# A state space layer with two states per scan instruction: a zero-decay column, an extra copy and fixed PSUM banks

## The chip, the cores and the metric

One of the eight cores of one Trainium2 chip runs the whole program. The metric is device time in microseconds (us), the median of several runs. Engines are named as the profile names them: PE (matmul), DVE (VectorE), ACT (ScalarE), POOL (GpSimd). Every kernel's time here is the median of four runs in the fast state, compared with runs of the kernel before on the same chip in the same rounds. The experiments ran on several chips; the kernel before took 8367 to 8369 us on each of them, so times of different experiments may be set side by side. The kernel places its tiles in one of two memories, SBUF or PSUM (`space=PSUM` in the code).

## The reference, cut to what matters

Two layers follow each other. The second (a windowed attention) is not touched by the change. The first is a selective state space layer over 4 sequences of 4096 positions, with 768 channels and 16 states per channel. Its heart is a recurrence along the sequence:

```python
def step(h, inp):
    dt_t, B_t, C_t, x_t = inp
    dA = jnp.exp(dt_t[:, :, None] * A[None])
    dBx = (dt_t * x_t)[:, :, None] * B_t[:, None, :]
    h = dA * h + dBx
    y_t = jnp.einsum('bdn,bn->bd', h, C_t)
    return (h, y_t)
```

## The kernel before

A sequence is cut into chunks of T = 256 positions, 64 chunks ("steps") in all. In a step 768 channels are 6 tiles of 128 partitions, and 16 states are 4 groups of 4: 24 groups (m) per step. A group is worked off in two halves of two states, so a step has 48 slots. The product dtx = dt * x is made by POOL, once per tile of channels and step; ACT copies it to PSUM (`dtx_ps`) for the products on DVE. The work of a group:

```python
def driven(I, m, h, eng):                 # db = dt * x * B, on DVE (15 of 24) or POOL (9 of 24)
    d, g = divmod(m, NS // NG)
    db = w2.tile([P, NG, T], F32, tag="db", name=f"db_{I}_{m}", bufs=6)
    dtx = dtx_ps[:, d % 2, :] if eng is nc.vector else h["dtx"][d]
    eng.tensor_tensor(db, dtx.unsqueeze(1).broadcast_to([P, NG, T]), h["B"][g], ALU.mult)
    dbs[I, m] = db

def decay(I, m, half, h):                 # da = exp(dt * A), on ACT into PSUM, two buffers
    d, g = divmod(m, NS // NG)
    da = ps_a.tile([P, 2, T], F32, tag="da", name="da")
    for k in range(2):
        n = g * NG + 2 * half + k
        act(da[:, k, :], h["dt"][d // 2][:, d % 2, :], AF.Exp, scale=nega[:, d, n : n + 1])
    das[I, m, half] = da

def scans(I, m, half, hs):                # h = da * h + db, on DVE, one state at a time
    ...
    for k in range(2):
        ...
        nc.vector.tensor_tensor_scan(hs[:, j, :], da[:, k, :], dbs[I, m][:, j, :],
                                     state[:, d, n : n + 1] if I % NCHUNK else 0.0, ALU.mult, ALU.add)

def with_c(I, m, h, hs):                  # last column kept as next chunk's start, then times C, on POOL
    d, g = divmod(m, NS // NG)
    nc.gpsimd.tensor_copy(state[:, d, g * NG : (g + 1) * NG], hs[:, :, T - 1])
    nc.gpsimd.tensor_tensor(hs, hs, h["C"][g], ALU.mult)
```

Everything else of the layer (projections, convolution, layer norm, softplus, gating) is hung into the 48 slots by hand-written tables. The order of instructions on each engine is exactly the order in which this loop writes them:

```python
for half in range(2):
    decay(*nxt, ...)                      # ACT: the decays of the next slot
    if half == 0:
        with_c(*behind[-1])               # POOL: the group before
        ...
    scans(I, m, half, hs)                 # DVE: this slot
    run(I, 2 * m + half, 2 * m + half + 1)   # whatever the tables put into this slot
```

Of the kernel before, what the change touches and what calls it, by code (L numbers as in the profile page):

```python
# [14 lines left out]
P = 128  # L15
C = 384
# [32 lines left out]
def two_layers(  # L49
# [221 lines left out]
    def layer0(x1s, mvs, gms1):  # L271

        with ExitStack() as es:
            es.enter_context(tc.manual_schedule(engines=in_step))
            ps_a = es.enter_context(tc.tile_pool(name="ps_a", bufs=2, space=PSUM))
            ps_x = es.enter_context(tc.tile_pool(name="ps_x", bufs=1, space=PSUM))
            ps_y = es.enter_context(tc.tile_pool(name="ps_y", bufs=1, space=PSUM))
            ps = es.enter_context(tc.tile_pool(name="ps0", bufs=4, space=PSUM))
            bc = es.enter_context(tc.tile_pool(name="bc", bufs=4))
            w1 = es.enter_context(tc.tile_pool(name="w1", bufs=1))  # L280
            w2 = es.enter_context(tc.tile_pool(name="w2", bufs=2))
            gms, gbs, st1s = {}, {}, {}
            dtx_ps = ps_x.tile([P, 2, T], F32, name="dtx_ps")

            def group_norm(b, mv):

# [15 lines left out]
            def next_batch(b, at):  # L302

                st = small.tile([P, NJ, NXT, 6], F32, tag="st0", name=f"st0_{b + 1}")
                mv = small.tile([P, NJ, 2], F32, tag="mv0", name=f"mv0_{b + 1}")
                h = {}

                def load(t, j):
                    h["x"] = w1.tile([P, TX], F32, tag="xs", name=f"xs_{b}_{t}_{j}")
                    nc.sync.dma_start(  # L310
                        h["x"], x[b + 1, j * P : (j + 1) * P, t * TX : (t + 1) * TX]
                    )

                def aggregate():
                    for j in range(NJ):
                        nc.vector.bn_aggr(mv[:, j, :], st[:, j, :, :])

                for n in range(NJ * NXT):
                    t, j = divmod(n, NJ)
                    at(24 * n + 14, lambda t=t, j=j: load(t, j))  # L320
                    at(24 * n + 26, lambda t=t, j=j: nc.vector.bn_stats(st[:, j, t, :], h["x"]))
                end = 24 * NJ * NXT + 24
                at(end, aggregate)
                for n, part in enumerate(group_norm(b + 1, mv)):
                    at(end + 2 + 3 * n, part)
# [4 lines left out]
            def normed(I, h, at):  # L330
# [38 lines left out]

                at(12, load)  # L370
                at(22, by_group)
                at(24, lambda: mean("xn", "mu"))
                at(26, lambda: with_row("mu", ALU.subtract))
                at(30, square)
                at(31, lambda: mean("sq", "var"))
                at(34, root)
                at(35, lambda: with_row("var", ALU.mult))

            def in_proj(pb, k, m, xn):

# [18 lines left out]
            def prepared(I, h, at):  # L399
# [19 lines left out]
                    for k in range(2):  # L419
                        at(slots[k], lambda k=k: one(k))  # L420

                at(-11, kept)
                for p, (x, c, z) in enumerate((
                    ((-10, -9, -6), (1, 2, 5), (9, 10, 13)),
                    ((-6, -5, -2), (3, 4, 7), (12, 13, 16)),
                    ((-4, -3, 0), (7, 8, 11), (15, 16, 19)),
                )):
                    d = 2 * p
                    pair(("x", p), x, lambda pb, k, d=d: in_proj(pb, k, d + k, h["xn"]))
                    at(x[2], lambda p=p, d=d: with_bias(  # L430
                        xb[:, d : d + 2, KC - 1 :], h["pb"][("x", p)], binp[:, d : d + 2]
                    ))

                    def conv_out(p=p, d=d):
                        c = w2.tile([P, 2, T], F32, tag="xc", name=f"xc_{b}_{i}_{d}", bufs=6)
                        with_bias(c, h["pb"][("c", p)], cvb[:, d : d + 2])
                        h["xc"].append(c)

                    pair(("c", p), c, lambda pb, k, d=d: conv(pb, k, d + k))
                    at(c[2], conv_out)  # L440

                    def z_out(p=p, d=d):
                        z = w2.tile([P, 2, T], F32, tag="sz", name=f"sz_{b}_{i}_{d}", bufs=6)
                        with_bias(z, h["pb"][("z", p)], binp[:, ND + d : ND + d + 2])
                        h["sz"].append(z)

                    pair(("z", p), z, lambda pb, k, d=d: in_proj(pb, k, ND + d + k, h["xn"]))
                    at(z[2], z_out)
# [27 lines left out]
                        nc.sync.dma_start(t, src.unsqueeze(0).broadcast_to([P, NG, T]))  # L476
                        h[tag].append(t)

                at(26, burst)
                at(28, lambda: x_proj((0, 1, 2)))  # L480
                at(29, lambda: x_proj((3, 4, 5)))
                at(32, rows)

                def softplus(q, first):

# [41 lines left out]
                    at(first + 6, lost)  # L527
                    at(first + 7, added)

                for q, first in enumerate((34, 36, 46)):  # L530
                    softplus(q, first)

            dbs, das = {}, {}

            def dt_x(I, d, h):
                h["dtx"][d] = w2.tile([P, T], F32, tag="dtx", name=f"dtx_{I}_{d}")
# [3 lines left out]
                )  # L540

            def dt_x_copied(d, h):
                nc.scalar.copy(dtx_ps[:, d % 2, :], h["dtx"][d])

            def driven(I, m, h, eng):

                d, g = divmod(m, NS // NG)
                db = w2.tile([P, NG, T], F32, tag="db", name=f"db_{I}_{m}", bufs=6)
                dtx = dtx_ps[:, d % 2, :] if eng is nc.vector else h["dtx"][d]
                eng.tensor_tensor(  # L550
                    db, dtx.unsqueeze(1).broadcast_to([P, NG, T]), h["B"][g], ALU.mult
                )
                dbs[I, m] = db

            def decay(I, m, half, h):

                d, g = divmod(m, NS // NG)
                da = ps_a.tile([P, 2, T], F32, tag="da", name="da")
                for k in range(2):
                    n = g * NG + 2 * half + k  # L560
                    act(da[:, k, :], h["dt"][d // 2][:, d % 2, :], AF.Exp, scale=nega[:, d, n : n + 1])
                das[I, m, half] = da

            def scans(I, m, half, hs):

                d, g = divmod(m, NS // NG)
                da = das.pop((I, m, half))
                for k in range(2):
                    j = 2 * half + k
                    n = g * NG + j  # L570
                    nc.vector.tensor_tensor_scan(  # L571
                        hs[:, j, :], da[:, k, :], dbs[I, m][:, j, :],
                        state[:, d, n : n + 1] if I % NCHUNK else 0.0,
                        ALU.mult, ALU.add,
                    )

            def with_c(I, m, h, hs):

                d, g = divmod(m, NS // NG)
                nc.gpsimd.tensor_copy(state[:, d, g * NG : (g + 1) * NG], hs[:, :, T - 1])  # L580
                nc.gpsimd.tensor_tensor(hs, hs, h["C"][g], ALU.mult)  # L581

            def summed(I, m, h, hs):


                d, g = divmod(m, NS // NG)
                if d % 2 == 0 and g == 0:
                    h["yt"][d // 2] = ps_y.tile([P, 2, 2, P], F32, tag="y", name="y")
                y = h["yt"][d // 2]
                for k in range(NG):  # L590
                    first = g == 0 and k == 0
                    last = g == NS // NG - 1 and k == NG - 1
                    for half in range(2):
                        nc.tensor.matmul(  # L594
                            y[:, d % 2, half, :], hs[:, k, half * P : (half + 1) * P], ident,
                            is_transpose=True, start=(first and half == 0 and d % 2 == 0),
                            stop=(last and half == 1 and d % 2 == 1), skip_group_check=True,
                        )

            def turn(I, p, h, at, s):  # L600


                def out():
# [21 lines left out]
                    h["yg"].append(yg)  # L625

                at(s, out)
                at(s + 1, back)
                at(s + 4, gated)

            def out_proj(I, h, at):
                b, i = divmod(I, NCHUNK)
# [34 lines left out]
                            nc.vector.bn_aggr(mvs[b][:, m, :], st1s[b][:, m, :, :])  # L667

                at(10, reload)
                for n, slot in enumerate((17, 18, 19, 20, 22, 23)):  # L670
                    m, part = divmod(n, 2)
                    at(slot, lambda m=m, part=part: tile_part(m, range(3 * part, 3 * part + 3)))
                at(26, lambda: residual(0, 2))
                at(28, lambda: residual(2, 1))
                at(30, stats)


# [6 lines left out]
            def slot_of(I):  # L684
# [7 lines left out]
            driven_at = (  # L692
                (-4, 0), (-1, 1), (1, 1), (2, 1), (4, 0), (7, 1), (8, 0), (10, 1),
                (12, 0), (15, 1), (17, 1), (18, 1), (20, 0), (22, 1), (24, 0), (26, 1),
                (26, 1), (26, 1), (30, 0), (33, 1), (36, 0), (39, 1), (40, 0), (43, 1),
            )
            dt_x_at = (-5, 2, 10, 18, 22, 34)

            for I in range(STEPS):
                h = steps[I]  # L700
                for p in range(ND // 2):
                    turn(I, p, h, slot_of(I), (p + 1) * (SLOTS // 3) + 4)
                out_proj(I, h, slot_of(I + 1))
                prepared(I, h, slot_of(I - 1))
                normed(I, h, slot_of(I - 2))
# [32 lines left out]
            behind = []  # L738
            for n in range(STEPS * M):
                I, m = divmod(n, M)  # L740
                hs = w2.tile([P, NG, T], F32, tag="hs", name=f"hs_{I}_{m}", bufs=5)
                for half in range(2):
                    if 2 * n + half + 1 < len(halves):
                        nxt = halves[2 * n + half + 1]
# [420 lines left out]
```

## Time and profile before

| | before |
|---|---|
| time, median | 8367 us |
| state space layer: one step of 64 | 92.3 us |
| attention layer, from 6020 us on | 2338 us |
| DVE busy in the layer, per step | 90.6 us (98%) |
| POOL, PE, ACT busy, per step | 84.9, 78.2, 72.6 us |

How the step and busy times are read, and the lines that they come from, stands in the prediction.

### The profile page before, as it was taken

To read this page: it belongs to the slowest core of one execution; us is meant where nothing else is said; L and a number is where in the kernel's file an instruction comes from. 1 tells how busy PE (TensorE), PEld (TensorE's weight loads), DVE (VectorE), ACT (ScalarE), POOL (GpSimd) and SP (SyncE) were. 2 spreads that over 40 slices of the span, in tenths; PEclk is the share of its full clock that TensorE was granted. 3 is DMA by queue.
4 is the path that set the end of the run, shared out by engine and by line. 5 is a ranking of instruction groups with operands and counts; after the bars stand their busy time and mean duration, and the time that the engine had idled before them with its cause. 6 is when DMAs were issued, how large, how long until landed. Compare 5 with 4: busy or idle time off the path is not lost. (4 is left out here: it accounts for less than half of the span.)

```text
span 8357.8 us, 139186 instructions
## 1 busy us (share of the span) xinstructions
PE 7252.0 (87%) x45882; PEld 5495.0 (66%) x45882; DVE 7311.7 (87%) x13300; ACT 5812.2 (70%) x13758; POOL 7092.7 (85%) x5719
## 2 busy tenths in 40 slices
PE   7888888888888888888888888888699999999999
PEld 5776677777666677776777677766555555555555
DVE  5999999999999999999999999999856666666666
ACT  5777777777777777777777777777545455455455
POOL 4999999999999999999999999999767677777677
PEclk9998898889889998899898889989799999999999
DMA  3111211121112111211211111112122232232222
GB/s 112 59 61 66 75 58 55 63 74 58 62 66 74 53 58 66 72 58 64 68 63 53 58 65 60 55 57 71 65 89 86 76 94 88 78 92 85 83 87 65
DMA packets 327504, 583.06 MB, mean 70 GB/s; under 512 B 62940, under 2 KB 211180, under 8 KB 326660
## 3 DMA queue, kind: packets, MB, share of 16 engines
q1 hardware_dynamic: 326788, 574.17, 21.3%
q8 instruction: 370, 6.06, 0.3%
q14 instruction: 346, 2.83, 0.1%
HBM read 471.49 MB, written 84.73 MB: 67 GB/s over the span
## 5 line engine op out<-in xcount | busy, mean ns | idle before, releaser
L571 DVE TENSOR_TENSOR_SCAN hs<-da,state,db 128x256 f32<-128x256 f32 x5760 | 3855.0, 728 | 88.9 <-ACT da L96 64.8
L96 ACT ACTIVATE da<-dt,nega 128x256 f32<-128x256 f32 x6144 | 2917.7, 477 | 1208.2 <-DVE hs L571 1100.8
L581 POOL TENSOR_TENSOR hs<-hs,C 128x1024 f32<-128x1024 f32 x1536 | 3621.7, 2358 | 123.9 <-POOL state L580 0.4
L594 PE MATMUL y<-ident,hs 128*128 128x128 f32 x12288 | 1774.6, 296 | 904.5 <-POOL hs L581 902.3
L594 PEld LDWEIGHTS y<-ident,hs 128*128 128x128 f32 x12288 | 1540.5, 153 | 1207.9 <-POOL hs L581 1098.9
L941 POOL TENSOR_SCALAR sg<-sg,rsum 128x308 f32<-128x308 f32 x1536 | 1619.9, 1073 | 633.8 <-DVE rsum L939 631.8
L550 POOL TENSOR_TENSOR db<-dtx,B 128x1024 f32<-128x1024 f32 x576 | 1360.5, 2362 | 0.1
L550 DVE TENSOR_TENSOR db<-dtx_ps,B 128x1024 f32<-128x1024 f32 x960 | 1141.3, 1199 | 0.0
L382 PE MATMUL mm_ps<-xn,w_in 128*128 128x256 f32 x4608 | 1127.4, 392 | 10.1 <-DVE yg L624 8.1
L96 ACT ACTIVATE sg<-sg,mx 128x308 f32<-128x308 f32 x1536 | 828.7, 541 | 251.3 <-DVE mx L926 236.7
L926 DVE CUSTOM_DVE_ANT_0 sg<-lg_ps,bias 128x308 f32<-128x308 f32 x1536 | 643.1, 475 | 375.1 <-PE lg_ps L920 375.1
L382 PEld LDWEIGHTS mm_ps<-xn,w_in 128*128 128x128 f32 x4608 | 872.5, 197 | 119.1 <-DVE yg L624 8.4
L389 PE MATMUL mm_ps<-xb,dcv 128*128 128x256 f32 x3072 | 783.9, 409 | 0.0
L389 PEld LDWEIGHTS mm_ps<-xb,dcv 128*128 128x128 f32 x3072 | 615.7, 208 | 88.3 <-issue 0.3
L969 ACT COPY tb<-pt_ps 88x512 f32<-88x512 f32 x384 | 222.2, 579 | 624.7 <-PE pt_ps L965 624.7
L580 POOL COPY state<-hs 128x4 f32<-128x4 f32 x1536 | 289.1, 188 | 341.8 <-DVE hs L571 328.0
L639 PE MATMUL mm_ps<-yg,w_out 128*128 128x256 f32 x2304 | 539.8, 385 | 0.0
L956 DVE COPY ta<-pt_ps 110x512 f32<-110x512 f32 x768 | 492.4, 682 | 23.2 <-PE pt_ps L951 23.2
L639 PEld LDWEIGHTS mm_ps<-yg,w_out 128*128 128x128 f32 x2304 | 439.6, 195 | 59.1
L951 PE MATMUL pt_ps<-ident,sg 128*110 128x128 f32 x3072 | 417.7, 279 | 0.8 <-POOL sg L941 0.8
L951 PEld LDWEIGHTS pt_ps<-ident,sg 128*110 128x110 f32 x3072 | 322.7, 133 | 77.9 <-issue 47.6
L824 PE MATMUL mm_ps<-xn,w_qkv 128*128 128x512 f32 (+2 forms) x612 | 270.7, 579 | 60.4 <-DVE xn L811 53.2
(141 smaller groups left out, 9152.5 us busy)
## 6 DMA issues: line engine op xcount, KB each, us to landing
B<-bcrows SPq DMA_DIRECT2D x256, 512.0 KB
C<-bcrows SPq DMA_DIRECT2D x256, 512.0 KB
vw<-vd SPq DMA_DIRECT2D x1792, 33.0 KB
xr<-x SPq DMA_DIRECT2D x28, 1056.0 KB
vd<-v SPq DMA_DIRECT2D x280, 96.0 KB
xi<-in_x_dram SPq DMA_DIRECT2D x64, 384.0 KB
xo<-in_x_dram SPq DMA_DIRECT2D x64, 384.0 KB
x<-xo SPq DMA_DIRECT2D x64, 384.0 KB
```

Of the source, the lines that this page charges most:

```text
L96: ins = nc.scalar.activation(o, i, func, **kw)
L382: nc.tensor.matmul(pb[:, k, :], w_in[:, j, m * P : (m + 1) * P], xn[:, j, :], start=(j == 0), stop=(j == NJ - 1),)
L389: nc.tensor.matmul(pb[:, k, :], dcv[:, d, c, :], xb[:, d, c : c + T], start=(c == 0), stop=(c == KC - 1),)
L550: eng.tensor_tensor(db, dtx.unsqueeze(1).broadcast_to([P, NG, T]), h["B"][g], ALU.mult)
L571: nc.vector.tensor_tensor_scan(hs[:, j, :], da[:, k, :], dbs[I, m][:, j, :], state[:, d, n : n + 1] if I % NCHUNK else 0.0, ALU.mult, ALU.add,
L581: nc.gpsimd.tensor_tensor(hs, hs, h["C"][g], ALU.mult)
L594: nc.tensor.matmul(y[:, d % 2, half, :], hs[:, k, half * P : (half + 1) * P], ident, is_transpose=True, start=(first and half == 0 and d % ...
L639: nc.tensor.matmul(h["po", first][:, m - first, :], w_out[:, d, m * P : (m + 1) * P], h["yg"][d // 2][:, d % 2, :], start=(d == 0), stop=( ...
L926: nc.vector.tensor_tensor_reduce(sg[:, hh, :], lg[:, :NK], bias[:, 4 * m + hh, :], -1.0, BIG, ALU.add, ALU.min, mx[:, hh : hh + 1],)
L941: nc.gpsimd.tensor_scalar(sg[:, hh, :], sg[:, hh, :], rs[:, hh : hh + 1], None, ALU.mult)
L951: nc.tensor.transpose(pt[: KN[c], col : col + P], sg[:, 2 * pair + hh, KOFF[c] : KOFF[c] + KN[c]], ident,)
L956: nc.vector.tensor_copy(t[: KN[0], :, :].rearrange("p a q -> p (a q)"), pt[: KN[0], :])
```

## The change

The change wants to pay half as often what a scan instruction costs beyond its columns: about 0.11 us, an estimate from two spacings of back-to-back scans, 0.645 us for 256 columns before and 1.18 for 513 in e1_defer. Two states are laid one behind the other with one column between them: a decay of 0 in that column wipes out the first state, and the drive (db) in that column holds the second state's starting value. One scan of 2 x 256 + 1 = 513 columns then does both. For that, the tiles get a gap of one column per pair, the starting value must be copied into each db, and a decay pair takes 513 columns of PSUM, one more than before. In the change each of the two pair buffers has a fixed tile of 4 x 256 columns, which it shares with a copy of dtx, and the pool for everything else shrinks from four buffers to three. A bank is here what the kernel's helper `bank` hands out, a PSUM tile of 2 x 256 columns; a fixed tile counts as two. Some slots were moved to fit the three banks.

```diff
-            ps = es.enter_context(tc.tile_pool(name="ps0", bufs=4, space=PSUM))
+            ps = es.enter_context(tc.tile_pool(name="ps0", bufs=3, space=PSUM))
+            pairs = [ps_a.tile([P, 4 * T], F32, name=f"pair_{k}") for k in range(2)]
+            dtx_ps = [t[:, 0:T] for t in pairs]
+            da_ps = [t[:, T : 3 * T + 1] for t in pairs]
+            for t in da_ps:
+                nc.vector.memset(t[:, T : T + 1], 0.0)
...             (driven)
-                db = w2.tile([P, NG, T], F32, tag="db", name=f"db_{I}_{m}", bufs=6)
+                db = w2.tile([P, 2, 2 * T + 1], F32, tag="db", name=f"db_{I}_{m}", bufs=6)
                 eng.tensor_tensor(
-                    db, dtx.unsqueeze(1).broadcast_to([P, NG, T]), h["B"][g], ALU.mult
+                    states(db), dtx.unsqueeze(1).unsqueeze(1).broadcast_to([P, 2, 2, T]),
+                    h["B"][g].rearrange("p (a k) t -> p a k t", k=2), ALU.mult,
                 )
+                kept = state[:, d, g * NG : (g + 1) * NG].rearrange("p (a k) -> p a k", k=2)
+                nc.scalar.copy(db[:, :, T : T + 1], kept[:, :, 1:2] if I % NCHUNK else zeros)
                 dbs[I, m] = db
...             (scans)
-                for k in range(2):
-                    ...
-                    nc.vector.tensor_tensor_scan(hs[:, j, :], da[:, k, :], dbs[I, m][:, j, :], ...)
+                nc.vector.tensor_tensor_scan(
+                    hs[:, half, :], da_ps[half], dbs[I, m][:, half, :],
+                    state[:, d, n : n + 1] if I % NCHUNK else 0.0, ALU.mult, ALU.add,
+                )
...             (tables: some 50 entries moved by one to seven slots, for example)
-                at(26, burst)
+                at(27, burst)
-                for q, first in enumerate((34, 36, 46)):
+                for q, first in enumerate((35, 37, 43)):
```

## The prediction

> **What bounds the kernel now.** I read the page first for the engines by time, then the stretches of the state space layer, then its groups, then the timeline.
>
> ```profile
> PE   7888888888888888888888888888699999999999
> DVE  5999999999999999999999999999856666666666
> ACT  5777777777777777777777777777545455455455
> POOL 4999999999999999999999999999767677777677
> ```
>
> Two layers: slices 1 to 29 are the state space layer (the scans start at 114 us and end at 6020 us), the rest is the attention, which the diff leaves alone. The first consists of 64 equal steps, (6020 - 114) / 64 = 92.3 us each. A stretch from its middle (columns: PE, PE weight load, DVE, ACT, POOL busy) says how full each engine is:
>
> ```profile
> 1000.00:3000.00 2000.00, 1694.25 (x8876) 1405.86 (x8875) 1963.95 (x2867) 1572.01 (x3442) 1838.58 (x1383) 0.89 0.19 64
> ```
>
> Per step: DVE 1963.95 / 2000 x 92.3 = 90.6 us, POOL 84.9, PE 78.2, ACT 72.6. DVE is the bound, with 1.7 us idle per step, and POOL is close. What fills them:
>
> ```profile
> L571 DVE TENSOR_TENSOR_SCAN hs<-da,state,db 128x256 f32<-128x256 f32 x5760 | 3855.0, 728 | 88.9 <-ACT da L96 64.8
> L96 ACT ACTIVATE da<-dt,nega 128x256 f32<-128x256 f32 x6144 | 2917.7, 477 | 1208.2 <-DVE hs L571 1100.8
> L581 POOL TENSOR_TENSOR hs<-hs,C 128x1024 f32<-128x1024 f32 x1536 | 3621.7, 2358 | 123.9 <-POOL state L580 0.4
> L550 POOL TENSOR_TENSOR db<-dtx,B 128x1024 f32<-128x1024 f32 x576 | 1360.5, 2362 | 0.1
> L550 DVE TENSOR_TENSOR db<-dtx_ps,B 128x1024 f32<-128x1024 f32 x960 | 1141.3, 1199 | 0.0
> ```
>
> A step has 24 groups of four states in 48 slots (half a group, two states). Per slot ACT makes two decays (da), DVE scans them. Per group DVE (15 of 24) or POOL (9 of 24) makes the scan's input db, and POOL multiplies the result by C. da has two buffers, so ACT is never more than one slot ahead. The timeline around slot 20:
>
> ```profile
> 3018.66 0.99 ACT L96 ACTIVATE da<-dt,nega 128x256 f32<-128x256 f32 x2 [0.67 <-DVE hs L571]
> 3018.69 0.19 POOL L580 COPY state<-hs 128x4 f32<-128x4 f32 x1
> ...
> 3018.96 2.36 POOL L581 TENSOR_TENSOR hs<-hs,C 128x1024 f32<-128x1024 f32 x1
> ...
> 3020.37 1.90 ACT L96 ACTIVATE da<-dt,nega 128x256 f32<-128x256 f32 x4
> 3021.29 2.36 POOL L550 TENSOR_TENSOR db<-dtx,B 128x1024 f32<-128x1024 f32 x1
> 3021.45 1.39 DVE L571 TENSOR_TENSOR_SCAN hs<-da,state,db 128x256 f32<-128x256 f32 x2 [0.25 <-POOL hs L581]
> ```
>
> Slot 19's scans end at about 3018.6; POOL then multiplies by C and only then makes a db, done at 3023.65, 5.05 us later. Nobody minds: that db is for four slots later, ACT has made the decays of slots 22 and 23 at 3020.37, and DVE scans slot 22 at 3021.45.
>
> [...] a scan of 256 that starts from a constant takes 667 ns, a tensor_tensor of 512 takes 666. [...] five scans take 3.29 us, (3.29 - 0.73) / 4 = 0.64 apart (0.645 over several such runs)[...]. [...] in 1000 to 6000 us ACT stands 40.7 us before dtx_ps for POOL's dtx, and no later instruction passes it. [...]
>
> **The change, part by part.** (1) Two scans of 256 become one of 513: [...] 1.181 us instead of 2 x 0.645 = 1.290. Saved 0.109 x 48 = 5.2 us a step, so DVE work goes from 90.6 to 85.4 (adding up its instructions at back-to-back spacings I get 86.4, and use that below). (2) POOL and DVE write and read tiles with a gap; counts and element numbers are unchanged, so I expect unchanged durations. (3) Moved slots and one PSUM bank less: PE has 14 us a step spare, I count nothing. (4) Each db gets its starting state by a copy of 128x2 on ACT, 24 a step, about 0.2 us each (from ACT operations on 32x1 at 0.20 to 0.24): 4.8 us of ACT work, which alone would do no harm.
>
> But where it stands does harm. In the built program's order the copy waits for the whole db of the same slot s, though it writes other columns, and the decays of slot s+2 stand behind it. So ACT, whose lead is one slot, now waits for a product that used to have several slots of time.
>
> POOL slots. From the end of scan s-1: 0.06 (semaphore: scan's end to state copy) + 4.96 (3018.69 to 3023.65 above) + 0.06 + 0.20 copy + 0.99 decays + 0.06 = 6.33 us until scan s+2 may start. In it DVE has two scans, 2.36, and what else stands in slots s-1 to s+1 (db 1.14 back to back, other operations from their rows: 0.66, 0.93, 1.05, 1.33 for two). Other ACT work between the copy and the decays adds to the chain. Chain minus cover: slot 4: 6.33 - 2.73 (statistics, 0.37 on average) = 3.6; slot 8: 7.15 (two activations, 0.82) - 3.5 (a db) = 3.65; 12: 6.33 - 3.02 (gating) = 3.3; 20: 6.33 - 2.36 = 3.95; 24: 6.33 - 3.02 (residual) = 3.3; 30: 7.15 (the square) - 3.4 (statistics) = 3.75; 36: 6.33 - 3.3 (layer norm) = 3.0; 40: 8.4 (softplus on ACT, 2.1) - 5.5 (a db, gating, softplus) = 2.9; 44: 6.33 - 5.5 (a db, softplus) = 0.8. Sum 28.3 us a step.
>
> DVE slots. The copy can start 0.06 after the db; copy and decays 1.25 later DVE has run one scan, 1.18: nearly even. With other ACT work behind the copy there is a stall: about 1.4 around slot 47 (softplus), 0.6 and 1.0 around slots 13 to 15, 0.6 at 33, 0.5 elsewhere. The worst is slot 27: two copies wait for two DVE products, and behind them stands the burst of table load, six Silu and table load, 5.8 us (3029.46 to 3035.28), which used to run beside three DVE products; then 0.99 of decays, against 0.93 + 0.37 + 1.18 of DVE work: 4.7 us. Sum 8.8.
>
> Step: 86.4 + 28.3 + 8.8 = 123.5; walking all 48 slots in order by hand with these durations gave 124.1. Difference to 92.3: 31.8 us, times 64 = 2035. 8366 + 2035 = 10,400 us.
>
> **The rivals.** A, the intended one: the copies cost nothing on the path and DVE stays the bound: 8366 - 64 x 5.2 = 8030. For it: DVE is 98% busy and every saved us counts now. Against: the waits above. B, POOL takes over: state copy plus product takes 2.60 (3018.69 to 3021.29), so 24 x 2.60 + 9 x 2.36 + 6 x 0.73 (dtx) = 88.0 a step; with 86 on DVE and few buffers between them I would take 88 to 90, 8090 to 8220. Same objection. C, only the DVE products' waits bite, because POOL's db comes in time: 86.4 + 8.8 = 95 a step, 8550. Against: slot 20 above, where POOL's db cannot start before the multiplication that needs scan s-1. D, the long scan over two PSUM banks or POOL on gapped tiles is slower than I assume: 0.1 us more per scan is 4.8 a step, some 300 us on top.
>
> **Range and chances.** The stall sum of 37 us rests on about 25 chains; I give it 4 to 6 us for latencies, the unseen copy and POOL's gapped access, times 64: 400 us either way. Range 10,000 to 10,850. The direction hangs on one reading, that ACT really stands before the POOL product: faster by over 2% 0.03, within 2% 0.03, slower 0.94.
>
> **What would show it.** A step near 124 us; DVE and POOL each about 69% busy in the layer, ACT near 62%. The scan's row: 3072 of 513 at about 1.25 us, some 2,300 us idle before it, ended by ACT. The new copy's row: 1536, some 0.2 us, about 22 us a step (1,400 in all) idle before it, ended by POOL db. POOL rows at 2.36 us. I am wrong if the copy's wait for POOL is small, or if the scan's mean is well over 1.3 us; the attention should keep its 2,330 us.

## The result, and the profile after

The changed kernel takes 10,202 us (median of 4 runs, 10,198 to 10,203), the kernel before 8367 us. The ratio is 1.219, with a 95% interval of 1.217 to 1.221; it is slower by 22%. Ratios here and below are the mean time of one kernel's fast runs over that of the other's fast runs of the same rounds, so not quite the ratio of the medians quoted.

The share of each engine in 40 equal slices of the changed kernel's span (tenths busy) answers to the four rows of before:

```profile
PE   6777767777777777777777777777776999999999
DVE  5777777777777777777777777777776666666666
ACT  4666666666666666666666666666664454545455
POOL 3666666666666666666666676666666676777777
```

In the state space layer, now nearly 31 slices long, no engine is above seven or eight tenths: no engine is full any more, and a chain of waits sets the time. One stretch of it in numbers (time; PE, PE weight load, DVE, ACT and POOL busy; granted clock, DMA share, GB/s):

```profile
1000.00:3000.00 2000.00, 1435.36 (x6754) 1155.53 (x6753) 1454.16 (x1396) 1233.01 (x3014) 1371.91 (x1053) 0.81 0.14 48
```

The first scan starts at 117.2 us, the last ends at 7856.4, so a step takes 120.9 us. DVE is busy for 1454.16 / 2000 x 120.9 = 87.9 us of it, 2.7 less than before, and idle for 33.0, which was 1.7. The attention layer takes 2344 us, about as before (2338). The groups of the changed kernel (busy us, mean ns; idle before, and who ended it):

```profile
L587 DVE TENSOR_TENSOR_SCAN hs<-pair,state,db 128x513 f32<-128x513 f32 x2880 | 3641.5, 1279 | 1890.9 <-ACT pair L96 1610.6
L600 POOL TENSOR_TENSOR hs<-hs,C 128x1024 f32<-128x1024 f32 x1536 | 3480.2, 2266 | 124.4 <-POOL state L596 1.6
L96 ACT ACTIVATE pair<-dt,nega 128x256 f32<-128x256 f32 x6144 | 2865.4, 474 | 202.7 <-DVE hs L587 99.5
...
L569 ACT COPY db<-state 128x2 f32<-128x2 f32 x1440 | 278.8, 194 | 2528.8 <-POOL db L563 1356.8
...
L563 POOL TENSOR_TENSOR db<-dtx,B 128x1024 f32<-128x1024 f32 x576 | 1354.4, 2351 | 0.1
...
L563 DVE TENSOR_TENSOR db<-pair,B 128x1024 f32<-128x1024 f32 x960 | 1153.7, 1208 | 53.5 <-ACT pair L96 52.9
```

Two columns have changed places. Before, ACT stood idle for 1208 us before its decays (1101 of them ended by DVE's scans), and DVE for 89 us before its scans: ACT ran ahead and stood at the end of its lead. Now it is 203 us before the decays and 1891 us before the scans (1611 of them ended by decays). What ACT waits for has moved to a new row, the copy of 128x2: 0.19 us of work and 2529 us of idle time before it. The list of waits over the whole run splits that by who ended it (total, times, longest; it counts the copies of the first chunk too):

```profile
DVE hs L587 <- ACT pair L96: 1718.6, 995, 5.9
ACT db L569 <- POOL db L563: 1445.0, 576, 3.9
ACT db L569 <- DVE db L563: 1238.5, 896, 2.6
```

All 576 copies behind a POOL product waited, 2.5 us each. The timeline at slot 20, the same place that the prediction shows for before:

```profile
4046.48 0.19 POOL L596 COPY state<-hs 128x4 f32<-128x4 f32 x1 [1.27 <-DVE hs L587]
4046.75 2.26 POOL L600 TENSOR_TENSOR hs<-hs,C 128x1024 f32<-128x1024 f32 x1
...
4048.45 0.38 ACT L550 COPY pair<-dtx 128x256 f32<-128x256 f32 x1
4048.86 1.23 DVE L587 TENSOR_TENSOR_SCAN hs<-pair,db 128x513 f32<-128x513 f32 x1 [1.20 <-ACT pair L550]
4048.97 2.36 POOL L563 TENSOR_TENSOR db<-dtx,B 128x1024 f32<-128x1024 f32 x1
...
4051.36 0.19 ACT L569 COPY db<-zeros 128x2 f32<-128x2 f32 x1 [2.54 <-POOL db L563]
4051.46 1.89 ACT L96 ACTIVATE pair<-dt,nega 128x256 f32<-128x256 f32 x4
...
4052.53 1.23 DVE L587 TENSOR_TENSOR_SCAN hs<-pair,db 128x513 f32<-128x513 f32 x1 [2.45 <-ACT pair L96]
```

The chain can be read from top to bottom: the end of slot 19's scan releases POOL (4046.48), POOL multiplies by C and then makes db (until 4051.33), that releases ACT's copy (4051.36), behind it stand the decays of slot 22 (4051.46, the first pair done at about 4052.45), and they release slot 22's scan (4052.53). From the end of slot 19's scan, 4046.42, that is 6.11 us; the prediction had 6.33. The line at 4048.86 shows a second, smaller wait that the prediction had not named: the scan of slot 21 waited 1.20 us for the copy of dtx, which now lies in its tile. Over the whole run DVE's scans wait 194 us for such copies.

### The profile page after: what moved, and what is told of

Same layout as the page of the kernel before. It is cut to its first block, busy times and chain, and to the rows that moved or that the text cites. A ratio compares the mean times of both kernels' runs of the same rounds, so it can differ in the third digit from the quotient of the medians.

```text
span 10201.6 us, 137884 instructions
## 1 busy us (share of the span) xinstructions
PE 7836.8 (77%) x45882; PEld 5838.4 (57%) x45882; DVE 7139.0 (70%) x10231; ACT 5944.6 (58%) x15294; POOL 6985.1 (68%) x5719
## 5 line engine op out<-in xcount | busy, mean ns | idle before, releaser
L587 DVE TENSOR_TENSOR_SCAN hs<-pair,state,db 128x513 f32<-128x513 f32 x2880 | 3641.5, 1279 | 1890.9 <-ACT pair L96 1610.6
L600 POOL TENSOR_TENSOR hs<-hs,C 128x1024 f32<-128x1024 f32 x1536 | 3480.2, 2266 | 124.4 <-POOL state L596 1.6
L96 ACT ACTIVATE pair<-dt,nega 128x256 f32<-128x256 f32 x6144 | 2865.4, 474 | 202.7 <-DVE hs L587 99.5
L616 PE MATMUL y<-ident,hs 128*128 128x128 f32 x12288 | 1980.3, 319 | 791.9 <-POOL hs L600 599.9
L616 PEld LDWEIGHTS y<-ident,hs 128*128 128x128 f32 x12288 | 1727.2, 167 | 1195.1 <-POOL hs L600 810.4
L569 ACT COPY db<-state 128x2 f32<-128x2 f32 x1440 | 278.8, 194 | 2528.8 <-POOL db L563 1356.8
L387 PE MATMUL mm_ps<-xn,w_in 128*128 128x256 f32 x4608 | 1322.3, 438 | 312.5 <-ACT xb L96 246.9
L563 DVE TENSOR_TENSOR db<-pair,B 128x1024 f32<-128x1024 f32 x960 | 1153.7, 1208 | 53.5 <-ACT pair L96 52.9
L464 PE MATMUL mm_ps<-xc,w_xp 128*56 128x256 f32 x768 | 284.0, 525 | 395.7 <-ACT xc L96 395.7
L661 PE MATMUL mm_ps<-yg,w_out 128*128 128x256 f32 x2304 | 536.9, 383 | 31.8 <-ACT sz L96 31.7
L544 POOL TENSOR_TENSOR dtx<-dt,xc 128x256 f32<-128x256 f32 x384 | 279.2, 727 | 278.6 <-DVE dt L525 278.6
```

What stands on the lines that cost most here:

```text
L96: ins = nc.scalar.activation(o, i, func, **kw)
L387: nc.tensor.matmul(pb[:, k, :], w_in[:, j, m * P : (m + 1) * P], xn[:, j, :], start=(j == 0), stop=(j == NJ - 1),)
L563: eng.tensor_tensor(states(db), dtx.unsqueeze(1).unsqueeze(1).broadcast_to([P, 2, 2, T]), h["B"][g].rearrange("p (a k) t -> p a k t", k=2) ...
L587: nc.vector.tensor_tensor_scan(hs[:, half, :], da_ps[half], dbs[I, m][:, half, :], state[:, d, n : n + 1] if I % NCHUNK else 0.0, ALU.mult ...
L600: nc.gpsimd.tensor_tensor(by_state, by_state, h["C"][g].rearrange("p (a k) t -> p a k t", k=2), ALU.mult)
L616: nc.tensor.matmul(y[:, d % 2, half, :], hs[:, k // 2, at : at + P], ident, is_transpose=True, start=(first and half == 0 and d % 2 == 0), ...
```

## The experiments

Twelve kernels ran. All are correct on these inputs and all their profiles are of the fast state. Runs e1 to e6 and e11 ask what the loss is made of, the others whether a version of this idea beats the kernel before.

### e1_defer: the copy three slots or one slot later

The theory is that the copy's place, and not the copy, is what costs. This run keeps every instruction and moves the copies.

```diff
-                kept = state[...]; nc.scalar.copy(db[:, :, T : T + 1], ...)     # in driven
+            def started(I, m): ... nc.scalar.copy(dbs[I, m][:, :, T : T + 1], ...)
+                    slot_of(I)(slot + (1 if vector else 3), lambda I=I, m=m: started(I, m))
```

> The changed kernel, but the scalar engine's copy of the starting state is put three slots later where GpSimd makes the db and one slot later where VectorE does, so that it no longer stands ahead of decays that are needed at once. Same instructions, another place. Theory W (the wait of the copy is the whole loss): the 28 us a step in which ACT stood before db falls below 4 us, DVE is busy about 95% or more, a step is 88 to 91 us, 8100 to 8300 us in all, 0 to 3% faster than before. Rival L (long scans over two banks, one PSUM bank less and the moved slots cost most of it): stays above 9000.

Measured: 8463 us, ratio 1.011 (1.010 to 1.013). Of the 1835 us lost, 1739 came back by moving 24 copies of two columns per step. ACT's waits before them fell to 129 us in the stretch from 1000 to 6000 us. But the expected gain over the kernel before is missing: it is 1.1% slower, not up to 3% faster. So theory W holds for nearly all of the loss of 22%, and something else takes what the merged scans should have saved: a step takes 93.8 us, not 88 to 91. Where DVE waits in that stretch:

```profile
DVE hs L592 <- ACT pair L96: 160.4, 265, 1.8
DVE hs L592 <- ACT pair L550: 126.2, 156, 1.3
DVE db L563 <- ACT pair L96: 58.1, 53, 1.4
```

### e3_defer_pool and e11_defer_vec: one kind of copy alone

The same edit with `(0 if vector else 3)` and with `(1 if vector else 0)`.

> Only the copies behind GpSimd's products (9 of 24 a step) are three slots later; those behind VectorE's products stay where the change has them. Theory W with the sums of the prediction: removes the 28 us a step of the GpSimd chains and leaves about 9 to 12, so a step of 95 to 101 us, 8550 to 8950 us. Rival V (the copies behind VectorE's products, which hold ACT 19 us a step in the trace, are as bad as GpSimd's): above 9300 us.

Measured: 8929 us, ratio 1.067. Moving POOL's nine copies alone gets 1273 us back, 19.9 us a step. It lies inside the expected 8550 to 8950 and rules out rival V.

> The counterpart of e3_defer_pool: only the copies behind VectorE's products are one slot later, those behind GpSimd's stay. Theory W: GpSimd's chain of about 6 us from one scan to the scan three slots on stays nine times a step; the trace of the changed kernel charges VectorE's copies with the smaller part, so 9550 to 9950 us. If the two kinds of copies were equally bad: near 9000.

Measured: 9877 us, ratio 1.180. Moving DVE's fifteen copies alone gets 326 us back, 5.1 us a step. The two gains add up to 1599 us, together they give 1739: what is under the longer wait shows only when that wait is gone. A reader of the waits list alone would have been misled here. It charges DVE's copies with 1238 us, nearly as much as POOL's 1445, but moving these copies alone gains only 326. The author's estimate of the reason, which no run tests by itself: ACT waits for a DVE product while DVE, the engine that it feeds, is busy with that product, and only what DVE then waits for ACT counts.

### e4_swap: the copy before the product

```diff
+                nc.scalar.copy(db[:, :, T : T + 1], kept[:, :, 1:2] if I % NCHUNK else zeros)
                 eng.tensor_tensor(states(db), ..., ALU.mult)
-                nc.scalar.copy(db[:, :, T : T + 1], kept[:, :, 1:2] if I % NCHUNK else zeros)
```

> The copy stays in its slot but is issued before the product db instead of after it, so the product waits for the short copy and not the copy for the long product. Theory W: no long wait stands before ACT; what remains is that VectorE's or GpSimd's product may wait for ACT to come to the copy, some tenths of a us for 15 of 24 groups: 8100 to 8450 us. If the loss were in the long scans, the banks or the slots: above 9000.

Measured: 8545 us, ratio 1.021 (1.019 to 1.023), outside the expected 8100 to 8450. Swapping two statements gets back 1657 us, so the direction of the wait was the fault. DVE's products now wait for the copy, 198 us in the stretch from 1000 to 6000 us, about 0.25 us each. That is the size that was expected; the range was missed because the gain over the kernel before is missing here as in e1_defer.

### e2_split: the change without its two main parts

Layout, banks, tables and slots as in the change, but two scans of 256 per half and no copies.

```diff
+                for k in range(2):
+                    n = g * NG + 2 * half + k
+                    cut = slice(k * (T + 1), k * (T + 1) + T)
+                    nc.vector.tensor_tensor_scan(hs[:, half, cut], da_ps[half][:, cut],
+                        dbs[I, m][:, half, cut], state[:, d, n : n + 1] ..., ALU.mult, ALU.add)
```

> The changed kernel with its layout, fixed banks, three-bank table and moved slots, but again two scans of 256 per half with their own starting states, and without the copies. Theory W: everything else of the change is about free, so within 1.5% of the kernel before, 8240 to 8490 us, DVE bound at 97 to 98%. Rival L: layout, banks or slots cost by themselves, over 8500 us.

Measured: 8562 us, ratio 1.023. Rival L was right about this part: what the change does around the scans costs 2.3% by itself, some 194 us or 3.0 us a step. Against it e1_defer, which has long scans and well-placed copies, is only 99 us faster, 1.5 us a step. DVE's work did fall as meant. The stretch from 1000 to 3000 us of e2_split, and then of e1_defer:

```profile
1000.00:3000.00 2000.00, 1639.39 (x8539) 1359.09 (x8538) 1910.66 (x2765) 1513.32 (x3313) 1728.87 (x1332) 0.88 0.19 62
```

```profile
1000.00:3000.00 2000.00, 1654.55 (x8723) 1374.75 (x8721) 1849.48 (x1802) 1594.61 (x3888) 1758.82 (x1357) 0.90 0.19 62
```

A step is 95.4 us in e2_split and 93.8 in e1_defer (first scan to last, divided by 64), so DVE is busy for 91.1 and 86.7 us. The scans saved 4.4 us of work a step, and 2.8 of them came back as idle time (4.3 against 7.1). The two runs differ in the copies too: no run has two scans of 256 and well-placed copies, so what the 24 copies themselves cost is not shown.

### e5_before_slots: only the moved slots and the smaller pool

The kernel before, with `bufs=3` for the pool and all slots of the change, nothing else.

> The kernel before with nothing of the change but its moved slots and the table of three PSUM banks instead of four; dtx keeps its own bank, decays their two rotating banks, contiguous tiles. What is open: e2_split, which has the whole change but long scans and copies, came out 2.3% slower than before (8562 against 8368). Theory B (the loss there is the shared tile: dtx lies in the tile of a decay, so copy, product, decay and scan wait for each other): this run is within 0.7% of before, 8310 to 8430. Rival S (the moved slots and the missing bank cost it): about as slow as e2_split, 8500 to 8600.

Measured: 8487 us, ratio 1.015 (1.013 to 1.016). Theory B had expected no loss, rival S all of it; neither is right. Slots and the missing bank cost 120 us, the rest of e2_split's 194 us, 75 us, comes with the layout and the shared tile. Slots and bank were changed together, so the run does not say which of the two it is: with three banks the slots of before were not tried. Its trace shows the added waiting around ACT: in 1000 to 6000 us DVE's scans wait 126 us for decays, which was 68, and ACT waits 146 us for dtx before its dtx copies, which was 41.

This run also separates an effect of layout. POOL's multiplication, in contiguous tiles at the slots of the change:

```profile
L581 POOL TENSOR_TENSOR hs<-hs,C 128x1024 f32<-128x1024 f32 x1536 | 3622.5, 2358 | 123.9 <-POOL state L580 0.2
```

It takes 2358 ns as before; in all runs with the gapped layout and dtx in PSUM that were read for it (the changed kernel, e1_defer, e2_split) it takes 2266 to 2273. Why is not shown.

### e6_split_parity and e7_defer_parity: keep dtx out of the way of the next decay

Five products and four dtx copies are moved by one slot, so that a product no longer reads the tile that the decays of the slot after next overwrite.

```diff
-                (-4, 0), (-1, 1), (1, 1), (2, 1), (4, 0), (7, 1), ...  (18, 1) ... (39, 1), (40, 0), (43, 1),
+                (-4, 0), (-1, 1), (1, 1), (3, 1), (4, 0), (6, 1), ...  (19, 1) ... (38, 1), (40, 0), (42, 1),
+            copied_at = (-2, 5, 12, 21, 24, 37)
```

> e2_split, with five of VectorE's products and four of the dtx copies moved by one slot, so that no product reads the tile which the decays of the next slot but one overwrite, and no copy goes into the tile that the next scan reads. Theory B: ACT's waits for a product (432 us in 5000) nearly vanish and the time falls by 80 to 200 us against e2_split, 8360 to 8480. Rival S: unchanged within 40 us of 8562.

Measured: 8565 us, no change from 8562. ACT's wait for the product, 432 us in 5000, is gone from the list, and the time did not move: theory B failed. In its place ACT waits longer for scans, 905 us instead of 587, so removing that wait by these moves gains nothing. DVE's waits in e6_split_parity, same stretch:

```profile
DVE db L563 <- ACT pair L96: 119.6, 250, 1.5
DVE hs L586 <- ACT pair L96: 62.6, 169, 0.9
```

They sum to 182 us. In e2_split it was 81 (scan for dtx copy) + 61 (scan for decay) + 46 (product for decay) = 188. In both runs somebody waits for the shared tile, and the moved slots only change whom.

> e1_defer with the same moves of products and dtx copies as e6_split_parity. Theory B: VectorE's idle time of 7 us a step halves, 8200 to 8330 us, faster than before by 0.5 to 2%. Rival S: 8420 to 8500 as e1_defer.

Measured: 8486 us, ratio 1.014, against 8463 of e1_defer; theory B failed again. The same picture: the scans no longer wait for the dtx copy, but the products now wait 149 us for decays, which was 58.

### e8_defer_sbuf: dtx from SBUF

```diff
-                dtx = dtx_ps[d % 2] if eng is nc.vector else h["dtx"][d]
+                dtx = h["dtx"][d]
-                    slot_of(I)(slot + 2, lambda d=d, h=h: dt_x_copied(d, h))
```

> e1_defer, but VectorE takes dtx from SBUF and the copies of dtx into PSUM are left out, so nothing but decays is in the paired banks. Theory B: the waits between copy, product, decay and scan are gone, 6 ACT copies a step less; 8150 to 8300 us if products of two SBUF operands neither get longer nor hold GpSimd up. If they do [...], the multiplication on GpSimd gets longer than 2.27 us on average and the time stays above 8350.

Measured: 9133 us, ratio 1.092, the second case of the expectation. The groups of e8_defer_sbuf:

```profile
L605 POOL TENSOR_TENSOR hs<-hs,C 128x1024 f32<-128x1024 f32 x1536 | 3606.6, 2348 | 123.8 <-POOL state L601 0.2
...
L563 DVE TENSOR_TENSOR db<-dtx,B 128x1024 f32<-128x1024 f32 x960 | 1908.3, 1993 | 0.0
...
L563 POOL TENSOR_TENSOR db<-dtx,B 128x1024 f32<-128x1024 f32 x576 | 1486.9, 2581 | 0.1
```

DVE's product took 1208 ns in e1_defer with one operand in PSUM and takes 1993 with both in SBUF, and POOL's product went from 2361 to 2581. The spread says more (shortest, median and longest in ns):

```profile
L563 DVE TENSOR_TENSOR db<-dtx,B x960: 1189/2094/3354, 112.7 to 6775.4; 128x1024 f32<-128x1024 f32 x192
```

At its shortest it is as short as with PSUM (1197 in the changed kernel), at its longest 2.2 us longer, about the time of one multiplication on POOL (2.27 in e1_defer). With both operands in SBUF the product costs 0.8 us more on average here; what holds it up is not shown. Of the two runs the one with dtx in PSUM is faster (8463 us against 9133), and there the change gives dtx no bank of its own: two pairs of two banks, one for y, three for the pool, as many in all as before.

### e9_defer_moved, e10_defer_moved14 and e12_lighter_act: trying to beat the kernel before

e9 moves three dtx copies and one product at the places where e1_defer's timeline shows DVE idle in every step; e10 also moves one POOL product two slots earlier; e12 takes 1.4 us a step of work off ACT.

```diff
-                (-4, 0), (-1, 1), (1, 1), ...  (24, 0), (26, 1),
+                (-4, 0), (-2, 1), (1, 1), ...  (22, 0), (26, 1),        # (22, 0) in e10 and e12 alone
+            copied_at = (-3, 5, 12, 21, 24, 37)
+            act(xb[:, d : d + 2, KC - 1 :], h["pb"][("x", p)], AF.Identity)   # e12 alone; z likewise
```

> e1_defer with four slots moved at the places where its trace shows VectorE idle in every step: three dtx copies one slot later (they held the next scan 0.62, 1.22 and 0.27 us), one VectorE product one slot earlier (it stood 1.08 us behind a decay of the same tile). If these are the stalls of e1_defer and no others take their place: 3.2 us a step, 8230 to 8330 us, about 1% faster than before. If ACT's lead of one slot is what is short, the stalls move on to the next ACT work and it stays at 8400 to 8480.

> As e9_defer_moved, with one GpSimd product (group 14) two slots earlier, so that its copy does not stand 0.67 us before the burst of Silu: another 20 to 60 us less than e9 if that stall is on the path, the same as e9 within 20 us if not.

> e10_defer_moved14 with less work on ACT: the in-projection's results x and z leave PSUM in one ACT instruction of 512 per pair of tiles, without bias, instead of two of 256 (0.58 against 0.82 us, six times a step, 1.4 us a step). It is right only because ln_b is zero in these inputs; it is made to weigh ACT's time, not to be kept. Theory A (what is left against the kernel before is ACT's short lead: decays and other ACT work no longer fit into the shorter slots): 40 to 110 us less than e10's 8460. If ACT's time is not on the path: within 20 us of it.

Measured: 8471 us, 8460 us and 8457 us, ratios 1.012, 1.011 and 1.010. e9 missed its first forecast; e10 is 11 us faster than e9, within the 20 that meant that its stall is not on the path. The stalls that e9 removed came back elsewhere. In e1_defer DVE waited 1.08 us at a product around slot 47; in e9's timeline, one step of it:

```profile
3973.92 2.46 DVE L592 TENSOR_TENSOR_SCAN hs<-pair,state,db 128x513 f32<-128x513 f32 x2 [1.24 <-ACT db L573]
...
4031.26 2.46 DVE L592 TENSOR_TENSOR_SCAN hs<-pair,state,db 128x513 f32<-128x513 f32 x2 [1.08 <-ACT pair L96]
...
4051.05 1.28 DVE L592 TENSOR_TENSOR_SCAN hs<-pair,state,db 128x513 f32<-128x513 f32 x1 [0.78 <-ACT pair L96]
```

The first now stands at a scan one slot on, and the one at 4031.26, behind the burst of Silu, grew from 0.73 to 1.08; the last stood in e1_defer already (0.79). All three are ended by ACT. That fitted a simple theory: slots have become 0.11 us shorter, ACT's lead is one slot, so ACT's other work no longer fits. e12 was to weigh that, and gave 3.5 us where 40 to 110 were expected. So ACT's time for x and z is not on the path, and the theory is not borne out; ACT's other work was not weighed. The large stalls left in one step of e12's timeline (1.23, 0.78 and twice 0.67 us) stand at softplus, at the burst and at a dtx copy that itself waits 1.16 us for POOL; e12 lightened none of these. What it would take to remove them was not tried. No version of the idea that was run beats the kernel before; the best is 1.0% slower, and 1.1% among those that do not rest on ln_b being zero.

## Why the prediction was right

The time was predicted at 10,400 us, in a range from 10,000 to 10,850, and is 10,202. Step by step:

- **The wait and its place.** Right, and shown by e1_defer, e3_defer_pool, e4_swap and e11_defer_vec: the copy's place is worth 1739 of 1835 us. The predicted 1,400 us of waiting before it for POOL's db are 1445 in the trace. DVE is 73% busy where 69% were expected, and the idle time before scans is 2,023 us (1,891 and, in the form without a state, 132) where 2,300 were.
- **The POOL chain.** 6.33 us were worked out, 6.11 measured at slot 20. The multiplication is 0.09 shorter than the row of before, and behind the copy the decays start after 0.10 us, not 0.20, because the next ACT instruction starts before the copy of 0.19 has ended. The sum of 28.3 us a step was over-sized: taking these waits away gains 19.9 us (alone) to 22.1 (after the others: 9877 to 8463 us, over 64).
- **The DVE slots.** 8.8 us predicted, 5.1 (alone) to 7.3 (after POOL's: 8929 to 8463 us, over 64) measured. It is the smaller part by a factor of three to four, as predicted. Its worst place, the burst of slot 27, was put at 4.7 us; in the changed kernel's timeline (at 4075.77 us) the scan behind the burst waits 4.48.
- **The scans.** The 1.181 us back to back was the author's estimate, and it was right: two take 2.46 in a timeline, one alone 1.28, so the second adds 1.18. Scans of 256 take 0.73 alone and 0.645 back to back; all these have a starting state from a tile. From the two spacings, (1.18 - 0.645) / 257 = 2.08 ns per column, which leaves 0.11 us per scan. The saving of 5.2 us of DVE work a step is 4.4 in e1_defer against e2_split. That DVE would then have nothing else to wait for was not claimed, and only 1.5 us of it reach the time.
- **Moved slots and one bank less: "I count nothing".** This step failed. It costs 120 us (e5_before_slots), 1.9 us a step. PE's spare time was the wrong thing to look at: the added waits in that trace are around ACT.
- **The layout: unchanged durations.** Nearly. DVE's product went from 1199 to 1208 ns, POOL's multiplication from 2358 to 2266. But the shared tile, for which the prediction counted nothing, adds waits of scans for dtx copies (194 us in the changed kernel); with the layout it costs about 75 us (e2_split against e5_before_slots).
- **The rivals.** A and B need the copy's wait to be free; with the copy well placed (e1_defer) neither 8030 nor 8090 to 8220 came about. C is refuted by e3 and e11; D finds no support, since scans take the predicted 1.18 us back to back and POOL's multiplication got faster (2266 ns, before 2358).

So the mechanism was right, and the closeness of the total is partly luck. The copies' waits were predicted at 37.1 us a step, and the copies' place is worth 27.2 (1739 / 64). The rest of the change was predicted at -5.3 (31.8, from the walk by hand, - 37.1) and is +1.5 (e1_defer against before, 95 / 64). The errors, -9.9 and +6.8, partly cancel, and leave 28.7 instead of 31.8.

Open remain: how the 120 us divide between slots and bank, how the 75 us divide between gap and shared tile, what the 24 copies themselves cost, and what removes the last stalls on ACT.

## What to carry to other kernels

When an engine gets a new small instruction, ask what it waits for and what stands behind it, not how long it takes: 24 copies of 0.19 us cost 27 us a step, because decays needed at once stood behind them (at slot 20 the copy waited 2.54 us, and the decays behind it started 0.10 us after it). Here ACT, whose lead is one slot, waited 2.5 us on average at each of 576 copies for a POOL product meant for four slots later; with the 24 copies issued later, when the product was due, and not when it was ordered, the time fell from 10,202 to 8463 us (e1_defer). And before crediting a saving on the busiest engine, check that whoever feeds it keeps up with the shorter beat: of 4.4 us saved, 1.5 arrived. Which waits took the rest was not settled here.
